# A four-layer graph stack on one core: a delayed linear map in layer 2, one added tile for its sums, small weights made in layer 0, and one running sum instead of two

## The chip, the cores and the metric

The kernel runs on one core of a Trainium2 chip. The metric is device time in microseconds (us) for one execution of the whole program. Two programs are compared: the kernel before and the changed one. A profile of one execution lies beside the times; its clock counts from the first to the last instruction.

## The reference, cut to what matters

`x` is 8 x 2048 x 64 in fp32; `adj` is a 2048 x 2048 row-normalised 0/1 graph. Four pre-norm layers each add something to `x`:

```python
def ln(x): return (x - mean(x, -1)) / sqrt(var(x, -1) + 1e-5)
# layer 0: weights per node n, made from a 16-wide embedding
h = max(ln(x), 0)
T = [h, A @ h, 2 * A @ (A @ h) - h]
w = einsum('nd,dkio->nkio', embedding, weight)      # 2048 x 3 x 64 x 64
x += einsum('bnki,nkio->bno', T, w) + embedding @ bias
# layer 1: three steps of a small network over v and A @ v
v = max(ln(x), 0); v[:, 0] = iv
for _ in range(3):
    v = relu(concat(v, A @ v) @ W1.T + b1) @ W2.T + b2
x += v
# layer 2: linear
h = max(ln(x), 0)
x += ((A @ h) * (w_nl.sum(-1) / sqrt(2)) + b_nl) @ w_out.T + b_out
# layer 3: attention masked by adj > 0.5; with no entry over 0.5
# every row's softmax is uniform, so each row gets the mean of h
h = max(ln(x), 0)
x += elu(mean over nodes of h)
```

## The kernel before, in words

**Two paths.** `uniform_path` computes under the assumption that all non-zero entries of a row of `adj` are equal and at most 0.5, and tests that assumption on the way. `general_path` follows under a branch and isn't taken with these inputs. Everything here is about `uniform_path`.

**Tiling.** Two batch entries of 64 channels form a pair of 128 columns; there are four pairs, `p` = 0 to 3. The nodes are cut into four blocks of 512, `nb` = 0 to 3. The sign of the transposed graph stays in SBUF as `BT`. A product with the graph (`product`, lines 170 to 182) takes one block: 16 chunks `m` of 128 nodes, each with a high and a low part of the operand (`H` and `L`, made by `halves`, lines 162 to 168), so 32 matmuls of 128 x 512 into one PSUM bank; VectorE then multiplies the bank by the row scale `crow` (line 181). `fill` lets a caller issue other work between chunks.

**Layer 0** runs per pair: four products for the first term, four for the second, and after each of these `node_weights` (lines 310 to 343). That function walks over 4 tiles `t` and two groups `dg` of 8 embedding entries. Per group TensorE makes `y` in PSUM (line 328, a tile of two banks, two such tiles), and VectorE adds each of its 8 slices times an embedding column to a sum (line 339). The kernel before keeps two sums: even entries go to `acc`, odd ones to `odd` (line 336 starts it), and line 342 adds them. `keep` then writes `x` to DRAM, normalises (`norm_relu`, lines 140 to 160) and writes `h` to DRAM.

**Norm.** `norm_relu` is a chain over three engines: VectorE sums, scales and subtracts the mean (145 to 147), ScalarE squares (151), VectorE sums and scales (153, 154), GpSimd takes the power -1/2 (156), VectorE applies it with the rectifier (157). Its output tile `z` shares a pool tag of 3 buffers with `hb`, the tile that `load_h` fills.

**Small weights.** After layer 0 its pools are closed. Lines 389 to 449 then load `W1`, `W2`, `w_out` and the vectors by some twenty DMAs on the SP queue into the same memory, transpose and multiply them on TensorE and copy them on VectorE.

**Layer 1** (515 to 565) has 3 steps of 4 products per pair; `back_to_nodes` (454 to 459, tile `bn`) applies a 128 x 128 matrix to a block. In its first two steps `test` (line 495) compares a quarter row of `adj` with the row's maximum; `test_load` fetches those quarters one call ahead into 4 buffers.

**Layer 2 and 3** (569 to 612) have one product per block and then `finish`: the GpSimd adds the bias row to `x` (578), `back_to_nodes` applies the matrix, VectorE adds (580), `norm_relu` follows, and four matmuls with a matrix of ones add the block's `z` over the nodes into the PSUM tile `pS` (583), over all four blocks. After the last block lines 602 to 612 turn `pS` into a row, add it to the four kept `acc` tiles and write the output through the POOL queue.

**Order.** The program is written for a tile framework: it assigns buffers and semaphores, and within each engine it orders the instructions by the place in the program at which they are issued and by its own estimate of when each is ready. So instructions may stand on an engine's queue later or earlier than the source has them[...].

Of the kernel before, what the change touches and what calls it, by code (L numbers as in the profile page):

```python
# [8 lines left out]
F32 = mybir.dt.float32  # L9
F32R = mybir.dt.float32r  # L10
I32 = mybir.dt.int32
U8 = mybir.dt.uint8
# [28 lines left out]
def uniform_path(  # L41
# [98 lines left out]
    def norm_relu(xt, name):  # L140
# [17 lines left out]
            g, g, 0.0, rstd[:, :, None].to_broadcast([P, 8, C]), op0=ALU.max, op1=ALU.mult  # L158
# [113 lines left out]

    l0p = l0.enter_context(tc.tile_pool(name="l0p", bufs=1))
# [36 lines left out]
    def node_weights(p, nb, terms):  # L310
# [3 lines left out]

        odd = l0p.tile([P, 4, 2 * C], F32, name="odd")
        av = acc.rearrange("p j (b c) -> p j b c", b=2)
        ov = odd.rearrange("p j (b c) -> p j b c", b=2)
# [3 lines left out]
        for t in range(4):  # L321
            ts = slice(t * P, (t + 1) * P)
            for dg in range(D // DG):
                y = psum.tile([P, 2, 512], F32, tag="big", name=f"y_{p}_{nb}_{t}_{dg}")
                for k in range(K):
                    for bb in range(2):
                        hs_ = slice(bb * C, (bb + 1) * C)
                        nc.tensor.matmul(  # L328
                            y[:, bb, :], terms[k][hs_, ts], wt[hs_, k, dg * 512:(dg + 1) * 512],
                            start=(k == 0), stop=(k == K - 1),  # L330
                        )
                for d in range(DG):
                    e = dg * DG + d
                    yd, ec = y[:, :, d * C:(d + 1) * C], emb[:, 4 * nb + t, e:e + 1]
                    if e == 1:
                        nc.vector.tensor_scalar(ov[:, t], yd, ec, None, op0=ALU.mult)
                        continue
                    xj = (av, ov)[d % 2][:, t]
                    nc.vector.scalar_tensor_tensor(  # L339
                        xj, yd, ec, xj, op0=ALU.mult, op1=ALU.add  # L340
                    )
        nc.vector.tensor_tensor(acc, acc, odd, op=ALU.add)
        keep(p, nb, acc, f"1_{p}_{nb}")

    for p in range(NP):
# [14 lines left out]
        for nb in range(NB):  # L360
            nm = f"0_{p}_{nb}b"
            crow = load_crow(nb, nm)
# [23 lines left out]
    def feat(name):  # L386
        return lastp.tile([P, 512], F32, tag="fm", name=name, bufs=8)

    def two_halves(src, width, name):
        t = lastp.tile([P, width], F32, name=name)  # L390
        for hf in range(2):
            nc.sync.dma_start(t[hf * C:(hf + 1) * C, :], src)
        return t

    def row(src, name):

        t = lastp.tile([P, 2 * C], F32, name=name)
        nc.sync.dma_start(
            t.rearrange("p (b c) -> p b c", b=2),
            bass.AP(tensor=src.tensor, offset=src.offset, ap=[[0, P], [0, 2], [1, C]]),  # L400
        )
        return t

    def block_diag(src, name):

        t = lastp.tile([P, P], F32, name=f"{name}n")
        nc.vector.memset(t, 0.0)
        for hf in range(2):
            s = slice(hf * C, (hf + 1) * C)
            nc.sync.dma_start(t[s, s], src)  # L410
        ps = bank("tr", f"ps_{name}")
        nc.tensor.transpose(ps[:, :P], t, ident)
        tT = lastp.tile([P, P], F32, name=name)
        nc.vector.tensor_copy(tT, ps[:, :P])
        return t, tT

    def made(name, lhsT, rhs, n=P):
        ps = bank("tr", f"ps_{name}")
        nc.tensor.matmul(ps[:, :n], lhsT, rhs, start=True, stop=True)
        t = lastp.tile([P, n], F32, name=name)  # L420
        nc.vector.tensor_copy(t, ps[:, :n])
        return t

    _, w1vT = block_diag(w1[:, :C], "w1v")
    _, w1eT = block_diag(w1[:, C:], "w1e")
    w2n, w2T = block_diag(w2, "w2")
    _, woT = block_diag(w_out, "wo")
    b1c = two_halves(b1[:, None], 1, "b1c")
    b2c = two_halves(b2[:, None], 1, "b2c")
    bnl = two_halves(b_nl[:, None], 1, "bnl")  # L430
    wn = two_halves(w_nl, 2, "wnl")
    b2r = row(b2, "b2r")
    bor = row(b_out, "bor")
# [3 lines left out]
    w1v2 = made("w1v2", w2n, w1vT)  # L437
    w1e2 = made("w1e2", w2n, w1eT)
    r1e = made("r1e", b2c.to_broadcast([P, P]), w1eT)
    b1s = made("b1s", w1vT, b2c, 1)  # L440
    nc.vector.tensor_tensor(b1s, b1s, b1c, op=ALU.add)

    rbo = made("rbo", bnl.to_broadcast([P, P]), woT)
    nc.vector.tensor_tensor(rbo, rbo, bor, op=ALU.add)
    ws = lastp.tile([P, 1], F32, name="wsum")
    nc.vector.tensor_scalar(wn, wn, INV_SQRT2, None, op0=ALU.mult)
    nc.vector.tensor_tensor(ws, wn[:, 0:1], wn[:, 1:2], op=ALU.add)
    wos = lastp.tile([P, P], F32, name="wos")
    nc.vector.tensor_scalar(wos, woT, ws, None, op0=ALU.mult)
# [32 lines left out]
    tested = []  # L482

    def test_load():
        for _ in range(2):
            i, q = divmod(len(tested), NB)
            st = lastp.tile([P, 512], F32, name="st", bufs=4)
            nc.sync.dma_start(st, adj[i * P:(i + 1) * P, q * 512:(q + 1) * 512])
            tested.append(st)

    def test(k):

        i, q = divmod(k, NB)
        junk = lastp.tile([P, 512], U8, name="junk")
        nc.vector.scalar_tensor_tensor(  # L495
            junk, tested[k], cols[:, i, :], tested[k], op0=ALU.not_equal, op1=ALU.logical_and,
            accum_out=bad[:, i, q:q + 1],
        )
# [16 lines left out]
    def layer1(n, p):  # L515
        hl, gT = ops[n]
        steps = 3
        for s in range(steps):
# [22 lines left out]
            for nb in range(NB):  # L541
# [3 lines left out]
                nc.tensor.matmul(ph, w1v2 if s else w1vT, gT[nb], start=True, stop=True)  # L545
                g = feat(f"g_{nm}")
                product(hl, nb, nm, g, crow, fill={8: mid} if nb == 3 else {})
                nc.vector.tensor_tensor(g, ph, g, op=ALU.add)  # L548
                nc.scalar.activation(g, g, AF.Relu, bias=b1s if s else b1c)  # L549
# [5 lines left out]
                if s < 2:  # L555
                    k = 2 * (8 * p + 4 * s + nb)
                    test(k)
                    test(k + 1)
                    if k + 2 < NCH * NB:
                        test_load()  # L560
# [8 lines left out]
    def layer2(n, p):  # L569
        hl, _ = ops[n]  # L570
        pS = bank("tr", f"pS_{p}")
        accs = []

        def finish(nb, e):
# [4 lines left out]
            pn = back_to_nodes(e, wos, f"2_{p}_{nb}")  # L579
            nc.vector.tensor_tensor(acc, pn, acc, op=ALU.add)  # L580
            z = norm_relu(acc, f"3_{p}_{nb}")
            for t in range(4):
                nc.tensor.matmul(  # L583
                    pS[:, :2 * C], ones, z[:, t, :],
                    start=(nb == 0 and t == 0), stop=(nb == NB - 1 and t == 3),
                )

        for nb in range(NB):
            nm = f"2_{p}_{nb}"
            crow = load_crow(nb, nm)  # L590
            e = product(
                hl, nb, nm, feat(f"e_{nm}"), crow,
                fill={8: lambda: prepare(n + 1, 2)} if nb == 3 else {},
            )
            finish(nb, e)
            if nb in (1, 2):
                prepare(n + 1, nb - 1)
        prepare(n + 1, 3)

# [14 lines left out]
    test_load()  # L614
# [599 lines left out]
```

## Time and profile before

| what | value |
|---|---|
| median of 3 runs | 1420.28 us |
| lowest and highest | 1418.68 and 1424.58 us |
| the profiled execution | 1418.68 us |
| its span, first to last instruction | 1416.9 us |
| TensorE matmul busy | 1277.4 us, 90% |
| VectorE busy | 805.6 us, 57% |
| GpSimd busy | 241.3 us, 17% |
| ScalarE busy | 187.4 us, 13% |
| mean granted TensorE clock | 0.962 |

In the profile PE is TensorE's matmul side and PEld its weight load, DVE VectorE, ACT ScalarE, POOL GpSimd, and SP the engine that issues most DMAs. A group line gives the source line, engine, operation, output and inputs, shape and count; after the first bar the busy time in us and the mean of one in ns; after the second the idle time of that engine just before, and what ended it. A timeline line gives start, duration, and in brackets the idle time before it with what ended it. Fp32 matmuls are recorded as two passes, so one call can show as two records.

By the timeline layer 0 with its prologue takes up to 720, the weights and the restart of layer 1 to 743, layer 1 to 1211, and layers 2 and 3 the rest.

### The profile page before, as it was taken

To read this page: it belongs to the slowest core of one execution; us is meant where nothing else is said; L and a number is where in the kernel's file an instruction comes from. 1 tells how busy PE (TensorE), PEld (TensorE's weight loads), DVE (VectorE), ACT (ScalarE), POOL (GpSimd) and SP (SyncE) were. 2 spreads that over 40 slices of the span, in tenths; PEclk is the share of its full clock that TensorE was granted. 3 is DMA by queue.
4 is the path that set the end of the run, shared out by engine and by line. 5 is a ranking of instruction groups with operands and counts; after the bars stand their busy time and mean duration, and the time that the engine had idled before them with its cause. 6 is when DMAs were issued, how large, how long until landed. Compare 5 with 4: busy or idle time off the path is not lost.

```text
span 1416.9 us, 16169 instructions
## 1 busy us (share of the span) xinstructions
PE 1277.4 (90%) x6000; PEld 899.3 (63%) x6000; DVE 805.6 (57%) x1956; ACT 187.4 (13%) x317; POOL 241.3 (17%) x234
## 2 busy tenths in 40 slices
PE   3899699997999799999949899999999999998883
PEld 2775355854566355755528687778778777776662
DVE  5655677476774777367757845334434433656553
ACT  3540001100100000000001112112112111101100
POOL 1200210212110211102010003002102201333442
PEclk9999899998999999999979999999999999999996
DMA  5771211211211211101027714103102211422220
GB/s 170 235 195 43 74 49 38 86 45 50 74 45 49 75 49 41 49 23 56 31 73 241 247 51 131 38 26 110 67 26 93 83 30 55 132 83 89 97 90 32
DMA packets 92299, 115.86 MB, mean 82 GB/s; under 512 B 50356, under 2 KB 52404, under 8 KB 92212
## 3 DMA queue, kind: packets, MB, share of 16 engines
q1 hardware_dynamic: 80052, 89.03, 21.2%
q0 software_dynamic: 7936, 24.66, 4.6%
q10 hardware_dynamic: 4224, 1.05, 0.3%
q8 instruction: 50, 0.82, 0.2%
q14 instruction: 37, 0.30, 0.1%
HBM read 90.05 MB, written 24.65 MB: 81 GB/s over the span
## 4 chain that ended last, share of the span: by engine, by line
PE 60%; DVE 10%; issue 10%; POOL 6%; DMA 4%; ACT 1%; SPq 1%; POOLq 0%; DVEq 0%; ACTq 0%
PE bv L175 23%; PE y L328 17%; POOL rstd L156 4%; PE bn L458 3%; PE ph L545 3%; DMA st<-in_adj_dram 2%; DVE z L157 2%; PE bv_3a L175 2%; PE bv_2a L175 2%; PE bv_0a L175 2%; PE bv_1a L175 2%; PE bv_0b L175 2%; POOL out_dram L609 1%; PE pS L583 1%; PE bn_u L458 1%
## 5 line engine op out<-in xcount | busy, mean ns | idle before, releaser
L175 PE MATMUL bv<-BT,H 128*128 128x512 f32 x1024 | 422.5, 413 | 0.0
L175 PE MATMUL bv<-BT,L 128*128 128x512 f32 x1024 | 406.2, 397 | 0.4 <-DVE L L167 0.4
L175 PEld LDWEIGHTS bv<-BT,L 128*128 128x128 f32 x1024 | 193.8, 189 | 49.9 <-issue 9.3
L175 PEld LDWEIGHTS bv<-BT,H 128*128 128x128 f32 x1024 | 193.6, 189 | 48.0 <-issue 9.3
L339 DVE SCALAR_TENSOR_TENSOR acc<-y,emb,acc 128x128 f32<-128x128 f32 x512 | 176.5, 345 | 79.7 <-PE y L328 75.3
L328 PE MATMUL y<-wt,t0T 64*128 64x512 f32 x512 | 145.1, 627 | 35.7 <-DVE odd L339 35.7
L339 DVE SCALAR_TENSOR_TENSOR odd<-y,emb,odd 128x128 f32<-128x128 f32 x448 | 153.7, 343 | 0.0
L306 POOL DMA_DIRECT2D xs<-acc x32 | 17.7, 554 | 781.1 <-DVE acc L528 347.9
L156 POOL TENSOR_TENSOR rstd<-var,mhalf 128x8 f32<-128x8 f32 x64 | 106.9, 1671 | 226.5 <-DVE var L154 199.1
L151 ACT ACTIVATE sq<-z 128x512 f32<-128x512 f32 x64 | 40.4, 631 | 627.5 <-DVE z L147 622.6
L157 DVE SCALAR_TENSOR_TENSOR z<-z,rstd 128x512 f32<-128x512 f32 x64 | 53.8, 840 | 107.9 <-POOL rstd L156 107.9
L328 PEld LDWEIGHTS y<-wt,t0T 64*128 64x128 f32 x512 | 46.3, 193 | 102.8 <-issue 101.1
L181 DVE TENSOR_TENSOR g<-bv,crow 128x512 f32<-128x512 f32 x48 | 33.1, 690 | 129.0 <-PE bv L175 128.7
L153 DVE TENSOR_REDUCE var<-sq 128x8 f32<-128x512 f32 x64 | 43.8, 684 | 28.5 <-ACT sq L151 28.5
L495 DVE SCALAR_TENSOR_TENSOR junk<-st,cols 128x512 uint8<-128x512 f32 x64 | 48.6, 759 | 14.4 <-DMA st<-in_adj_dram 13.0
L188 PE MATMUL pt_adj<-ident,st 128*128 128x128 f32 x256 | 39.5, 303 | 16.6 <-DMA st<-in_adj_dram 8.5
L224 DVE TENSOR_REDUCE cols<-st 128x1 f32<-128x1024 f32 x32 | 38.9, 1217 | 23.2 <-DMA st<-in_adj_dram 23.1
L188 PEld LDWEIGHTS pt_adj<-ident,st 128*128 128x128 f32 x256 | 31.8, 155 | 25.8 <-ACT BT L223 15.3
L583 PE MATMUL pS<-z,ones 128*128 128x128 f32 x128 | 20.4, 307 | 30.0 <-DVE z L157 30.0
L549 ACT ACTIVATE g<-g,b1s 128x512 f32<-128x512 f32 x32 | 23.2, 724 | 174.8 <-DVE g L548 174.8
L145 DVE TENSOR_REDUCE mean<-acc 128x8 f32<-128x512 f32 x64 | 43.4, 684 | 4.4 <-DMA acc<-in_x_dram 2.9
L147 DVE TENSOR_TENSOR z<-acc,mean 128x512 f32<-128x512 f32 x64 | 44.1, 694 | 1.7
(186 smaller groups left out, 1841.1 us busy)
## 6 DMA issues: line engine op xcount, KB each, us to landing
st<-in_adj_dram SPq DMA_DIRECT2D x32, 512.0 KB, 4.5
crow<-crowD SPq DMA_DIRECT2D x64, 256.0 KB, 3.3
st<-in_adj_dram SPq DMA_DIRECT2D x64, 256.0 KB, 3.4
hs<-z POOLq DMA_DIRECT2D x44, 256.0 KB, 2.7
hb<-hs SPq DMA_DIRECT2D x44, 256.0 KB, 4.0
xs<-acc POOLq DMA_DIRECT2D x32, 256.0 KB, 2.5
acc<-xs SPq DMA_DIRECT2D x32, 256.0 KB, 3.7
acc<-in_x_dram SPq DMA_DIRECT2D x56, 128.0 KB, 2.7
```

The lines of the kernel that those rows point to most:

```text
L145: nc.vector.tensor_reduce(mean, groups(xt), axis=AX.X, op=ALU.add)
L147: nc.vector.tensor_tensor(g, groups(xt), mean[:, :, None].to_broadcast([P, 8, C]), op=ALU.subtract)
L153: nc.vector.tensor_reduce(var, groups(sq), axis=AX.X, op=ALU.add)
L156: nc.gpsimd.tensor_tensor(rstd, var, mhalf, op=ALU.pow)
L157: nc.vector.scalar_tensor_tensor(g, g, 0.0, rstd[:, :, None].to_broadcast([P, 8, C]), op0=ALU.max, op1=ALU.mult)
L175: nc.tensor.matmul(ps, hl[m // 4][i][:, m % 4, :], BT[:, nb, m, :], start=(m == 0 and i == 0), stop=(m == NCH - 1 and i == 1),)
L188: nc.tensor.transpose(pt[:, t, :], src(t), ident)
L328: nc.tensor.matmul(y[:, bb, :], terms[k][hs_, ts], wt[hs_, k, dg * 512:(dg + 1) * 512], start=(k == 0), stop=(k == K - 1),)
L339: nc.vector.scalar_tensor_tensor(xj, yd, ec, xj, op0=ALU.mult, op1=ALU.add)
L458: nc.tensor.matmul(ps[:, t, :], fT[:, t * P:(t + 1) * P], wmat, start=True, stop=True)
L495: nc.vector.scalar_tensor_tensor(junk, tested[k], cols[:, i, :], tested[k], op0=ALU.not_equal, op1=ALU.logical_and, accum_out=bad[:, i, q: ...
L545: nc.tensor.matmul(ph, w1v2 if s else w1vT, gT[nb], start=True, stop=True)
```

## The change

- `node_weights`: the tile `odd`, its start (336) and the added line 342 go. All 16 entries of a tile `t` are added to the one slice `av[:, t]`, in order.
- The small weights are made by a new function `make_weights`, called in layer 0 for the last pair ahead of the second product of block 1. It uses three `z` buffers, and writes its eight 128 x 128 results to DRAM (`wD`) by two DMAs on the POOL queue. After layer 0 one DMA of 512 KB brings them into `wl`; two loads of `iv` and one row `b2r` stay there. `b1c` is loaded ahead of `make_weights`.
- `test` takes a whole row block: four loads, each followed by its comparison, into 2 buffers, at blocks 0 and 2 of the first two steps; the loads one call ahead go.
- Layer 1 keeps the product in a tile of its own (`e`) ahead of the activation. The tag `fm` has 10 buffers where it had 8.
- Layer 2: `finish(nb - 1)` and a later `prepare` are issued after chunk 4 inside the product of block `nb`. The block's `z` no longer goes through line 583: for block 0 `norm_relu` writes into `zsum`, and for blocks 1 to 3 VectorE adds `z` to it. After the last block four matmuls with ones add up `zsum`.

```diff
 def norm_relu(xt, name, out_=None):
...
-            g, g, 0.0, rstd[:, :, None].to_broadcast([P, 8, C]), op0=ALU.max, op1=ALU.mult
+            g if out_ is None else groups(out_), g, 0.0,
+            rstd[:, :, None].to_broadcast([P, 8, C]), op0=ALU.max, op1=ALU.mult,
...
+    def make_weights():
+        b2c = col(b2[:, None], 1, "b2c")
+        bnl = col(b_nl[:, None], 1, "bnl")
+        wn = col(w_nl, 2, "wnl")
...
+        raw, tr, pr = (block("z", f"wz{i}", 3) for i in range(3))
+        nc.gpsimd.memset(raw, 0.0)
+        for i, w in enumerate((w1[:, :C], w1[:, C:], w2, w_out)):
+            for hf in range(2):
+                hs_ = slice(hf * C, (hf + 1) * C)
+                nc.sync.dma_start(raw[hs_, i, hs_], w)
+        nc.vector.tensor_copy(tr, transposed(lambda t: raw[:, t, :], "wT"))
+        ps = psum.tile([P, 4, P], F32, tag="tr", name="wP")
...
+        for i, (lhsT, rhs) in enumerate(pairs):
+            nc.tensor.matmul(ps[:, i, :], lhsT, rhs, start=True, stop=True)
+        nc.vector.tensor_copy(pr, ps)
...
+        fill_row(raw[:, 0, :], b_out)
+        nc.vector.tensor_tensor(pr[:, 3, :], pr[:, 3, :], raw[:, 0, :], op=ALU.add)
...
+        nc.gpsimd.dma_start(wD[:, 0], tr)
+        nc.gpsimd.dma_start(wD[:, 1], pr)
...
-        odd = l0p.tile([P, 4, 2 * C], F32, name="odd")
...
+                xj = av[:, t]
                 for d in range(DG):
                     e = dg * DG + d
-                    yd, ec = y[:, :, d * C:(d + 1) * C], emb[:, 4 * nb + t, e:e + 1]
-                    if e == 1:
-                        nc.vector.tensor_scalar(ov[:, t], yd, ec, None, op0=ALU.mult)
-                        continue
-                    xj = (av, ov)[d % 2][:, t]
                     nc.vector.scalar_tensor_tensor(
-                        xj, yd, ec, xj, op0=ALU.mult, op1=ALU.add
+                        xj, y[:, :, d * C:(d + 1) * C], emb[:, 4 * nb + t, e:e + 1], xj,
+                        op0=ALU.mult, op1=ALU.add,
                     )
-        nc.vector.tensor_tensor(acc, acc, odd, op=ALU.add)
...
+            if p == NP - 1 and nb == 1:
+                make_weights()
...
+    wl = lastp.tile([P, 2, 4, P], F32, name="wl")
+    nc.sync.dma_start(wl, wD)
...
+    def test(i):
+        for q in range(NB):
+            st = lastp.tile([P, 512], F32, name="st", bufs=2)
+            nc.sync.dma_start(st, adj[i * P:(i + 1) * P, q * 512:(q + 1) * 512])
+            junk = lastp.tile([P, 512], U8, name="junk")
+            nc.vector.scalar_tensor_tensor(
...
-            z = norm_relu(acc, f"3_{p}_{nb}")
-            for t in range(4):
-                nc.tensor.matmul(
-                    pS[:, :2 * C], ones, z[:, t, :],
-                    start=(nb == 0 and t == 0), stop=(nb == NB - 1 and t == 3),
-                )
+            z = norm_relu(acc, f"3_{p}_{nb}", zsum if nb == 0 else None)
+            if nb > 0:
+                nc.vector.tensor_tensor(zsum, zsum, z, op=ALU.add)
+
+        def behind(nb):
+            if nb > 0:
+                finish(nb - 1)
+            if nb > 1:
+                prepare(n + 1, nb - 2)
 
         for nb in range(NB):
...
+            fill = {4: lambda: behind(nb)}
+            if nb == 3:
+                fill[8] = lambda: prepare(n + 1, 2)
+            e.append(product(hl, nb, nm, feat(f"e_{nm}"), crow, fill=fill))
+        finish(3)
         prepare(n + 1, 3)
+        pS = bank("tr", f"pS_{p}")
+        for t in range(4):
+            nc.tensor.matmul(pS[:, :2 * C], ones, zsum[:, t, :], start=(t == 0), stop=(t == 3))
```

## The prediction

> **What bounds the kernel now.** I read the groups first, then busy time by stretch, then the timelines of TensorE and VectorE. The groups that the change touches (busy us, mean ns, then idle before it and what ended that):
>
> ```profile
> L339 DVE SCALAR_TENSOR_TENSOR acc<-y,emb,acc 128x128 f32<-128x128 f32 x512 | 176.5, 345 | 79.7 <-PE y L328 75.3
> L328 PE MATMUL y<-wt,t0T 64*128 64x512 f32 x512 | 145.1, 627 | 35.7 <-DVE odd L339 35.7
> L583 PE MATMUL pS<-z,ones 128*128 128x128 f32 x128 | 20.4, 307 | 30.0 <-DVE z L157 30.0
> ```
>
> In `node_weights` VectorE waits for TensorE's `y` (75.3 us), hardly the other way. In layer 2 it is reversed: TensorE sits idle 30.0 us ahead of the `pS` matmuls, for the norm's last step. By stretch (window, length, then busy us of PE, PEld, DVE, ACT, POOL, clock, DMA):
>
> ```profile
> 610.74:631.68 20.94, 20.94 (x98) 9.58 (x97) 15.82 (x57) 0.00 (x0) 0.00 (x0) 1.00 0.04 14
> 717.80:743.40 25.60, 4.71 (x15) 3.17 (x15) 11.17 (x39) 0.93 (x2) 4.05 (x4) 0.60 0.30 94
> 1210.90:1400.50 189.60, 157.41 (x779) 126.59 (x778) 106.33 (x180) 20.48 (x35) 71.29 (x63) 0.96 0.26 85
> ```
>
> A block's `y` stage is all TensorE (20.94 of 20.94). Between layers 0 and 1 TensorE works 4.71 of 25.60 us. In layer 2 it lacks 32 of 189.6 us. How VectorE's instructions follow each other is what decides; this is its timeline in that `y` stage and at the end of layer 0:
>
> ```profile
> 657.87 0.35 DVE L339 SCALAR_TENSOR_TENSOR acc<-y,emb,acc 128x128 f32<-128x128 f32 x1 [0.46 <-PE y L328]
> 658.13 0.34 DVE L336 TENSOR_SCALAR odd<-y,emb 128x128 f32<-128x128 f32 x1
> 658.39 0.34 DVE L339 SCALAR_TENSOR_TENSOR acc<-y,emb,acc 128x128 f32<-128x128 f32 x1
> ...
> 719.57 0.34 DVE L339 SCALAR_TENSOR_TENSOR odd<-y,emb,odd 128x128 f32<-128x128 f32 x1
> 719.95 0.69 DVE L342 TENSOR_TENSOR acc<-acc,odd 128x512 f32<-128x512 f32 x1
> 720.68 0.69 DVE L145 TENSOR_REDUCE mean<-acc 128x8 f32<-128x512 f32 x1
> ```
>
> Alternating sums start 0.26 us apart although each lasts 0.343: the next starts ahead of the end. Line 342 reads what the instruction before it wrote, and line 145 does too: each starts 0.03 to 0.04 after that end. And layer 2's norm on VectorE:
>
> ```profile
> 1339.02 0.69 DVE L580 TENSOR_TENSOR acc<-bn,acc 128x512 f32<-128x512 f32 x1 [1.34 <-PE bn L458]
> 1342.12 0.69 DVE L153 TENSOR_REDUCE var<-sq 128x8 f32<-128x512 f32 x1 [0.76 <-ACT sq L151]
> 1344.84 1.75 DVE L157 SCALAR_TENSOR_TENSOR z<-z,rstd 128x512 f32<-128x512 f32 x1 [1.82 <-POOL rstd L156]
> 1346.51 1.28 DVE L167 TENSOR_TENSOR L<-hb,H 128x512 fp32r<-128x512 f32 x2
> 1348.07 0.69 DVE L181 TENSOR_TENSOR e<-bv,crow 128x512 f32<-128x512 f32 x1 [0.28 <-PE bv L175]
> ```
>
> The chain takes 7.57 us (1339.02 to 1346.59), of which 2.6 are waits for ScalarE and GpSimd. The product's scaling `e` stands behind it.
>
> **What the Trainium skill says.** "VectorE: DVE Perf Modes", section "The DRAIN you can't avoid": the next op waits for the pipe to empty, a semaphore adds nothing, but one that isn't held starts earlier. The trace agrees with the last clause (0.26 us apart at 0.343 long) and not with the second: a dependent start costs 0.12 us more. "SBUF — State Buffer" states in its single rule on ports that VectorE and GpSimd share a port pair exclusively, and that an op with two SBUF inputs contends. The trace agrees: line 157 lasts 0.69 us alone and 1.75 where GpSimd's line 578 (1344.78, 1.26 us) runs. "TensorE: Matmul & The Clock Gate", Part 1, says that about 3.4 us of idling halves the clock; here after a gap of 3.41 us at 1329 matmuls come 0.43 us apart, not 0.228.
>
> **Part 1, one running sum.** 16 instructions of a tile `t` now each read the one before. A dependent start gives 0.343 + 0.035 = 0.378 us; a group of 8 takes 3.03 us where TensorE makes one in 20.94 / 8 = 2.62. So VectorE becomes the bound of the stage. With two `y` tiles TensorE runs two groups ahead, then goes at VectorE's pace: 2.62 + 6 x 3.03 + 2.62 = 23.4 us a block, 2.5 more. VectorE then finishes 3.3 us later than now, less 0.73 for line 342; the norm behind it takes about 5.8 us, so the next product's scaling, queued behind the norm, is late for a 7.5 us product by some 0.4. I replayed the queue order of the trace with both costs: 2.75 to 2.93 more per block, 45.7 over 16. I take **+46**. Bounds: if dependent starts were free, nothing but the 0.73 us of line 342, mostly behind products (-2); if other work never overlaps, 16 x 8 x 0.41 = +52.
>
> **Part 2, layer 2.** The 16 groups of `pS` become 4. One costs TensorE 0.91 us (1255.34 to the next product matmul at 1256.25): 12 x 0.91 = 11 off its queue. Idle time up to the last `bn` is 25.5 us, matmuls at the halved clock another 8.5. If all goes, TensorE needs 32 x 0.2285 + 0.91 + 0.23 = 8.5 us a block against (1393.6 - 1212.0) / 16 = 11.35 now: -45. But VectorE comes next: chain 7.57, the added sum 0.72, its share of lines 602 to 607 (3.75 / 4), so 9.2 us a block even if `e` and line 167 fit in the 1.82 us wait; line 578 still follows `rstd` on POOL, so the 1.75 stays. 16 x (11.35 - 9.2) = -34. The output's eight POOL DMAs (6.0 us) of one pair meet the next pair's `rstd`: I charge 4 us in all. **-30**; bounds -38 (contention mostly gone) and -12 (`e` stays behind `z` and the added sum: 9.2 + 0.7 + 0.7 = 10.6 a block).
>
> **Part 3, weights.** After layer 0 SP issues 16 fewer small loads of about 0.63 us and one row fewer. The restart waits for the first `hb`: issued at 733.73, landed at 743.04, behind two rows of 64 KB that took 5.6 and 8.0 us to land. Now `wl`, two `iv`, one row: about 2.4 us of issue from 720.1, so `hb` goes at 722.5 not 733.7; the row remains ahead, so I keep 7 to 8 us to landing: 730. **-13** (-8 to -16). TensorE's and VectorE's removed steps lay inside that gap: nothing more.
>
> **Part 4, the same weights inside layer 0.** TensorE gets some 18 records of 0.11 us, 2 us; VectorE two copies of 0.69 and five small ones, 2.6, where Part 1 has made it the bound. Two waits are new on VectorE's queue, with `y` sums behind: `pr` needs a `z` buffer whose DMA (2.5 us) must end, and the `b_out` row must land (5.6 us for a row like it). I charge half of these, 3.5. POOL's memset and two DMAs stand in idle POOL time (21 us gaps). SP's loads are issued during a 21 us `y` stage; the `crow` load behind them has that cover, and without it costs up to 8. **+6** (+2 to +14).
>
> **Part 5, tests.** 64 comparisons remain. Two buffers instead of four: a load lands in 3.5 us, so about 2.3 us a test rather than 1.2, and VectorE's queue waits behind each. Before, TensorE lost 2.69 and 2.89 us here. **+2** (-4 to +12). **Tail:** the added sum lies on the last chain, +0.7. The tile `e` in layer 1 adds no instruction.
>
> **Sum:** 46 - 30 - 13 + 6 + 2 + 1 = +12. From the profiled 1418.7 that is 1430.7; the median lies 1.6 higher, so 1432.
>
> **Rivals.** (a) *Layer 2 becomes TensorE's alone*: the scaling moves into the `rstd` wait and GpSimd's add leaves line 157; -38 in place of -30, with the weights at -14 and little stall: about 1421, no change. For it: 1.82 us of bare wait in each norm; against: line 578 comes straight after `rstd`. (b) *New waits*: `e` stays behind the added sum (-15) and the tests or `b_out` hold VectorE's queue (+10 more): about 1452. For it: waits in queue order cost 30 us now. (c) **Faster**: the dependent chain in `node_weights` is cheaper than a dependent start elsewhere, because VectorE finds the other norms' instructions to put between. Place: line 339; price: at 0.34 us apart a group takes 2.72 us and Part 1 falls to about 16 x (6 x 0.10 + 0.4) = 16, so 1402. It decides from 0.36 us apart downward, where Part 1 is under 34. Against it: the chain's groups follow each other with nothing else ready in pair 3. (d) The change doing nothing is excluded: `pS` records must fall by 96.
>
> **Chances.** Forecast 0.45 (1422 to 1442), (a) 0.22, (b) 0.18, (c) 0.15. Within 0.5%, about what a measurement here tells from no change, is 1413 to 1427: (a), with a little of the forecast and less (c): 0.26. Faster 0.15, slower 0.59. The range reaches to the middle of (c) and just past that of (b), 1402 to 1455, and so leaves out about half of each, 0.17.
>
> **What would show it.** Line 339 starting 0.38 us apart with TensorE waiting for it over 100 us (Part 1); `y` stages of 23 to 24 us; few gaps before `pS`, layer 2 ending its last `bn` some 150 us after its start (Part 2); the first `pt` of layer 1 about 13 us after the last `y`, not 25 (Part 3); idle VectorE ended by `b_out`'s DMA (Part 4). Starts 0.26 us apart in line 339 would break the forecast.

## The result and the profile after

| | before | after |
|---|---|---|
| median | 1419.48 us | 1468.05 us |
| lowest and highest | 1414.11 and 1424.58 us | 1467.40 and 1475.08 us |
| span of the profiled execution | 1416.9 us | 1465.5 us |

These are four runs of each; the median of before stood at 1420.28 when there were three. The ratio of the times is 1.0354, with a 95% interval of 1.0304 to 1.0404: the change makes the kernel 3.5% slower. The forecast was 1432 with a range up to 1455, so the sign was right and the size was not: 48.6 us of span came where the sum said 12.

The spans can be cut at the same instructions in both traces (last `y` matmul, first transpose of layer 1, last linear map `bn` of layer 1, last `bn` of layer 2):

| stage | before | after | difference | the sum said |
|---|---|---|---|---|
| up to the first `y` matmul's end | 121.1 | 120.3 | -0.8 | 0 |
| layer 0, to the last `y` | 596.6 | 654.2 | +57.6 | +52 (Parts 1 and 4) |
| between layers 0 and 1 | 25.7 | 14.3 | -11.4 | -13 (Part 3) |
| layer 1 | 471.4 | 481.4 | +10.0 | +2 (Part 5) |
| layer 2, to the last `bn` | 179.0 | 171.4 | -7.6 | -30 (Part 2) |
| behind the last `bn` | 23.0 | 23.8 | +0.8 | +1 (tail) |

Two rows miss by much: layer 2 by 22 us and layer 1 by 8. Layer 0 misses by 6. First the groups on the page of the kernel after, in the same columns as before:

```profile
L383 DVE SCALAR_TENSOR_TENSOR acc<-y,emb,acc 128x128 f32<-128x128 f32 x1024 | 355.3, 350 | 62.8 <-PE y L376 20.2
L376 PE MATMUL y<-wt,t0T 64*128 64x512 f32 x512 | 149.1, 646 | 68.1 <-DVE acc L383 65.1
L482 DVE SCALAR_TENSOR_TENSOR junk<-st,cols 128x512 uint8<-128x512 f32 x64 | 48.6, 759 | 48.4 <-DMA st<-in_adj_dram 47.9
```

The wait between the two engines has turned round: VectorE now waits 20.2 us for `y` (75.3 before), TensorE 65.1 us for VectorE (35.7 before). The third line is the tests of layer 1: VectorE stands 47.9 us for their inputs, where it stood 13.0 before.

VectorE's part of one block of layer 0, where nothing else stands between:

```profile
648.31 24.58 DVE L383 SCALAR_TENSOR_TENSOR acc<-y,emb,acc 128x128 f32<-128x128 f32 x64 [2.10 <-PE y L376]
```

The same 64 instructions took 20.3 us before (613.63 to 633.94 in its timeline), and line 342 another 0.7. The busy time by stretch, in the columns of the forecast's table, for the `y` stage of that block, the stretch between the layers and layer 2:

```profile
645.42:669.76 24.34, 22.49 (x98) 9.63 (x97) 20.06 (x57) 0.00 (x0) 0.00 (x0) 1.00 0.04 12
774.50:788.80 14.30, 0.00 (x0) 0.00 (x0) 5.97 (x16) 0.93 (x2) 4.06 (x4) 0.67 0.52 153
1266.30:1448.30 182.00, 149.97 (x683) 120.88 (x682) 112.29 (x191) 19.72 (x35) 71.75 (x63) 0.92 0.27 89
```

The `y` stage grew from 20.94 to 24.34 us and TensorE lacks 1.85 of it. In layer 2 TensorE had 32.2 us idle before (189.60 less 157.41) and has 32.0 now (182.00 less 149.97): the forecast had most of that idle time go, and none did. What went is TensorE's own work, the 96 records of `pS`.

What TensorE waits for between the two `bn` marks shows where the wait is now. Before:

```profile
PE pS L583 <- DVE z L157: 23.4, 15, 3.4
PE bn L458 <- DVE e L181: 1.9, 2, 1.2
```

After:

```profile
PE bn L452 <- DVE e L182: 19.5, 9, 4.1
PE bv L176 <- DVE L L168: 4.7, 1, 4.7
PE pS L585 <- DVE zsum L566: 0.9, 1, 0.9
```

The columns are us in total, times, longest. The 23.4 us ahead of `pS` are gone but for 0.9, and 19.5 us ahead of `bn`, for the scaling `e`, and one wait of 4.7 us for `L` stand in their place. The timeline of VectorE in the last pair of the kernel after, with GpSimd's addition of the bias row put in at its time, says why:

```profile
1424.99 0.17 DVE L154 TENSOR_SCALAR var<-var 128x8 f32<-128x8 f32 x1
1426.91 1.26 POOL L561 TENSOR_TENSOR acc<-acc,wl 128x512 f32<-128x512 f32 x1
1426.97 1.74 DVE L157 SCALAR_TENSOR_TENSOR z<-z,rstd 128x512 f32<-128x512 f32 x1 [1.82 <-POOL rstd L156]
1428.64 0.68 DVE L182 TENSOR_TENSOR e<-bv,crow 128x512 f32<-128x512 f32 x1
1429.24 0.68 DVE L566 TENSOR_TENSOR zsum<-zsum,z 128x512 f32<-128x512 f32 x1
1430.63 0.69 DVE L563 TENSOR_TENSOR acc<-bn,acc 128x512 f32<-128x512 f32 x1 [0.72 <-PE bn L452]
```

TensorE had ended that product's matmuls at 1423.9 and the first ten of the next product, which stand ahead of `bn` on its queue, at 1426.2. Then it could go no further:

```profile
1429.37 0.82 PE L452 MATMUL bn<-wl,e 128*128 128x128 f32 x5 [3.21 <-DVE e L182]
```

The scaling could have run from 1423.9 and starts at 1428.64: it stands behind line 157, which first waits 1.82 us for GpSimd's `rstd` and then takes 1.74. That closes a loop: `e` of a block behind the norm of the block before it on VectorE, `bn` behind `e`, and the next norm behind `bn`. The one wait of 4.7 us for `L` has the same origin: line 168 (167 before), which makes it, starts at 1350.57, behind a line 157 that had waited 1.82 us for `rstd` and taken 1.74 (from 1348.18).

### The profile page after: what moved, and what is told of

It reads as the page before. It is cut to its first block, busy times and chain, and to the rows that moved or that the text cites. A ratio compares the mean times of both kernels' runs of the same rounds, so it can differ in the third digit from the quotient of the medians.

```text
span 1465.5 us, 15962 instructions
## 1 busy us (share of the span) xinstructions
PE 1292.0 (88%) x5904; PEld 893.5 (61%) x5904; DVE 878.3 (60%) x1941; ACT 186.7 (13%) x317; POOL 243.3 (17%) x237
## 3 DMA queue, kind: packets, MB, share of 16 engines
q1 hardware_dynamic: 80196, 89.55, 20.1%
## 4 chain that ended last, share of the span: by engine, by line
PE 35%; DVE 24%; issue 17%; DMA 8%; POOL 6%; ACT 1%; DVEq 0%; POOLq 0%; SPq 0%; ACTq 0%
PE bv L176 19%; DVE acc L383 15%; DMA st<-in_adj_dram 6%; POOL rstd L156 4%; PE bn L452 3%; PE y L376 3%; PE ph L532 2%; DVE junk L482 2%; PE bv_0a L176 2%; PE bv_1a L176 1%; PE bv_3a L176 1%; PE bv_2a L176 1%; PE bv_0b L176 1%; DVE mean L145 1%; DVE var L153 1%
## 5 line engine op out<-in xcount | busy, mean ns | idle before, releaser
L176 PE MATMUL bv<-BT,H 128*128 128x512 f32 x1024 | 422.4, 413 | 0.3 <-ACT H L167 0.3
L383 DVE SCALAR_TENSOR_TENSOR acc<-y,emb,acc 128x128 f32<-128x128 f32 x1024 | 355.3, 350 | 62.8 <-PE y L376 20.2
L376 PE MATMUL y<-wt,t0T 64*128 64x512 f32 x512 | 149.1, 646 | 68.1 <-DVE acc L383 65.1
L182 DVE TENSOR_TENSOR e<-bv,crow 128x512 f32<-128x512 f32 x64 | 44.1, 689 | 124.3 <-PE bv L176 124.2
L482 DVE SCALAR_TENSOR_TENSOR junk<-st,cols 128x512 uint8<-128x512 f32 x64 | 48.6, 759 | 48.4 <-DMA st<-in_adj_dram 47.9
L452 PE MATMUL bn<-wl,g 128*128 128x128 f32 x384 | 51.6, 277 | 7.9 <-ACT g L536 7.3
L452 PEld LDWEIGHTS bn<-wl,g 128*128 128x128 f32 x384 | 49.4, 192 | 14.0 <-ACT g L536 10.3
L189 PEld LDWEIGHTS pt_adj<-ident,st 128*128 128x128 f32 x256 | 32.0, 155 | 25.6 <-ACT BT L224 15.4
L536 ACT ACTIVATE g<-e,b1s 128x512 f32<-128x512 f32 x32 | 23.2, 724 | 165.2 <-DVE e L534 165.1
```

What stands on the lines that cost most here:

```text
L176: nc.tensor.matmul(ps, hl[m // 4][i][:, m % 4, :], BT[:, nb, m, :], start=(m == 0 and i == 0), stop=(m == NCH - 1 and i == 1),)
L182: nc.vector.tensor_tensor(out, ps, crow, op=ALU.mult)
L189: nc.tensor.transpose(pt[:, t, :], src(t), ident)
L376: nc.tensor.matmul(y[:, bb, :], terms[k][hs_, ts], wt[hs_, k, dg * 512:(dg + 1) * 512], start=(k == 0), stop=(k == K - 1),)
L383: nc.vector.scalar_tensor_tensor(xj, y[:, :, d * C:(d + 1) * C], emb[:, 4 * nb + t, e:e + 1], xj, op0=ALU.mult, op1=ALU.add,)
L452: nc.tensor.matmul(ps[:, t, :], fT[:, t * P:(t + 1) * P], wmat, start=True, stop=True)
```

## Experiments

Times are medians beside the kernel before on the same chip, with the ratio to it. "More" and "less" than the changed kernel compare with its median of 1468.05, which was not measured beside them; the kernel before, which was, has medians between 1418.2 and 1421.1 us there. Only `u_sum`, `l2_dep` and the three kernels put together have intervals clear of the changed kernel's (1.0304 to 1.0404). For the others the stretches of the traces, one profiled execution each, have to carry the reading. "Idle" is TensorE's, between the two `bn` marks of layer 2.

### Layer 0: is it the dependency?

`u_sum`: the two sums back, nothing else.

```diff
-                xj = av[:, t]
...
+                    xj = (av, ov)[d % 2][:, t]
...
+        nc.vector.tensor_tensor(acc, acc, odd, op=ALU.add)
```

> The changed kernel with the sum over a node's neighbours in layer 0 put back into two sums, neighbours taken alternately, and the adding of the two put back too; all else as changed. Theory (each of the 16 multiply-adds reads the sum that the one ahead of it wrote, and waits for that): the y stages of layer 0 fall from about 24.5 to about 21 us, the starts of the multiply-adds stand 258 ns apart and not 386, and 48 us go: about 1420. Rival (VectorE is bound by how many instructions it has, or by what they read, so one sum costs no more than two): no change or slower, 1468 to 1475.

Measured: 1412.62 us, ratio 0.9945 (0.9924 to 0.9967). On its page:

```profile
L389 DVE SCALAR_TENSOR_TENSOR acc<-y,emb,acc 128x128 f32<-128x128 f32 x512 | 175.9, 344 | 78.7 <-PE y L378 72.1
L378 PE MATMUL y<-wt,t0T 64*128 64x512 f32 x512 | 146.9, 626 | 36.1 <-DVE odd L389 36.1
```

VectorE waits 72.1 us for `y` again, and the median distance of two starts is 258 ns. The stretches of `y` matmuls (cut where they pause over 5 us) take 372.6 us together, 422.4 in the changed kernel, 366.3 before. That is 50 us for the one sum; all of layer 0 gives 51 (603.0 and 654.2), the medians 55. All the rest of the change together makes the kernel 0.3 to 0.8% faster.

`u_split`: two sums, but eight neighbours in a row to each.

```diff
-                xj = av[:, t]
...
+                    if e == DG:
...
+                    xj = (av, ov)[dg][:, t]
...
+        nc.vector.tensor_tensor(acc, acc, odd, op=ALU.add)
```

> The changed kernel with two sums in layer 0, but the first eight neighbours go to one and the last eight to the other, so that every multiply-add but one still follows the one whose sum it reads; the two are added at the end. Theory of the dependency: the starts stay 386 ns apart, and the time is 1460 to 1480. Rival (two tiles by themselves, or less in one tile, are what made the kernel before quick): about 1420, as with alternate sums.

Measured: 1482.24 us, ratio 1.0427 (1.0390 to 1.0465). Its timeline:

```profile
505.43 0.35 DVE L386 TENSOR_SCALAR odd<-y,emb 128x128 f32<-128x128 f32 x1
505.81 2.67 DVE L389 SCALAR_TENSOR_TENSOR odd<-y,emb,odd 128x128 f32<-128x128 f32 x7
508.52 0.69 DVE L392 TENSOR_TENSOR acc<-acc,odd 128x512 f32<-128x512 f32 x1
```

Seven take 2.67 us: (2.67 - 0.35) / 6 = 0.387 us apart, as with one sum (median 386 ns in both). The same instructions on the same two tiles go at 258 or at 386 ns by order alone. So it is the reading of the sum just written, and the rival (two tiles by themselves) falls. Whether the program's semaphore or the engine itself holds the second instruction is not shown. The time lies 14 us over the changed kernel and 2 over the expected range; the added line, 16 x 0.7 = 11 us, is most of the 14.

### Layer 1: two buffers

`t_bufs4`: four buffers for the tests' inputs, and one `fm` buffer fewer for room.

```diff
-    return lastp.tile([P, 512], F32, tag="fm", name=name, bufs=10)
+    return lastp.tile([P, 512], F32, tag="fm", name=name, bufs=9)
...
-            st = lastp.tile([P, 512], F32, name="st", bufs=2)
+            st = lastp.tile([P, 512], F32, name="st", bufs=4)
```

> The changed kernel with four buffers in place of two for the input lists that the tests of layer 1 read, paid for with one output buffer fewer. Theory (with two buffers VectorE waits 48 us for the transfers in layer 1, 13 us before, and that is most of the 10 us that layer 1 grew): 6 to 10 us less, about 1459. Rival (what costs is where in VectorE's order the tests stand, or the second half of the setup that waits behind them): no change, 1465 to 1471.

Measured: 1462.28 us, ratio 1.0301 (1.0266 to 1.0336), 5.8 us less than the changed kernel. VectorE's waits in layer 1:

```profile
DVE junk L482 <- DMA st<-in_adj_dram: 16.2, 19, 3.2
```

They were 47.9. Layer 1 takes 474.0 us where it took 481.4, so the buffers are 7.4 of its 10.0 (in the kernels with two buffers it takes 480.8 to 484.7, in the four with four 473.1 to 475.8). The other 2.6 were not pursued.

### The weights

`u_w`: the weights made behind layer 0 again, `make_weights` and `wD` gone.

```diff
-            if p == NP - 1 and nb == 1:
-                make_weights()
...
+    _, w1vT = block_diag(w1[:, :C], "w1v")
...
+    wos = lastp.tile([P, P], F32, name="wos")
+    nc.vector.tensor_scalar(wos, woT, ws, None, op0=ALU.mult)
```

> The changed kernel with the later weights made after layer 0 again, as in the kernel before (one output buffer fewer, for room). By the traces the junction between the layers fell by 11 to 14 us and layer 0 grew by 6 to 8: 3 to 8 us more than the changed kernel, 1471 to 1476. Rival (making them inside layer 0 costs as much as it saves): 1465 to 1470.

Measured: 1475.79 us, ratio 1.0395 (1.0354 to 1.0435), 7.7 us more than the changed kernel. The stretch between the layers is 23.9 us, against 14.3 in the changed kernel and 11.3 to 12.6 in the other kernels with early weights. The `y` stage that holds `make_weights` takes 32.7 us in the changed kernel and 24.7 here; with two sums it is 27.0 against 21.2. So the early weights save 10 to 13 between the layers and cost 6 to 8 in that stage. Over all of layer 0 the two profiles differ by only 1.6 us (654.2 and 652.6), so what they cost outside that stage is not pinned down. The two waits that the forecast named, in the changed kernel's timeline:

```profile
682.59 0.69 DVE L305 COPY wz<-pt_wT 128x512 f32<-128x512 f32 x1 [2.58 <-PE pt_wT L189]
685.75 0.69 DVE L311 COPY wz<-wP 128x512 f32<-128x512 f32 x1 [2.47 <-DMA hs<-z]
```

The wait for a `z` buffer came (2.47 us); the one for the `b_out` row did not, and one for the transposes (2.58 us) stood in its place.

### Layer 2: which wait holds it?

`u_l2`: layer 2 of the kernel before in the changed kernel.

```diff
-            fill = {4: lambda: behind(nb)}
...
+            finish(nb, e)
+            if nb in (1, 2):
+                prepare(n + 1, nb - 1)
```

> The changed kernel with layer 2 of the kernel before (each block's linear map and norm straight after its own product, the sums of h by TensorE after each block). From the traces, layer 2 and the tail fell by about 7 us with the change, where the prediction said 29. If that reading is right: 5 to 9 us slower than the changed kernel, 1473 to 1477. Rival (the new order gains what was predicted, and something else in the changed kernel lies on layer 2 and hides it): about 1497.

Measured: 1476.41 us, ratio 1.0422 (1.0377 to 1.0466), 8.4 us more. Its layer 2 takes 181.8 us, against 171.4. The new layer 2 is worth 8 to 10 us, and nothing else hides a larger gain.

`l2_noadd`: one link of the loop shortened, by leaving the row out.

```diff
-            nc.gpsimd.tensor_tensor(acc, acc, rows4(rbo), op=ALU.add)
```

> The changed kernel without GpSimd's addition of the row of w_out and b_nl in layer 2, so that the output lacks that row: one link of the chain from norm to norm is shortened, since the last multiplication of the norm takes 1.75 us where that addition lies on it and 0.69 where it doesn't. Theory (layer 2 is held by the loop of scaling, linear map and norm, TensorE waits 19.5 us in it): 8 to 15 us less, 1453 to 1460. Rival (layer 2 is held by the loads of x and of the counts, or by TensorE itself): 1464 to 1470.

Measured: 1454.81 us, ratio 1.0265 (1.0222 to 1.0308), 13.2 us less. Line 157 takes 0.69 us in each of layer 2's norms; in the changed kernel nine of the 16 take 1.74 to 1.78. TensorE's waits for `e` fall from 19.5 to 10.4 us. That fits the loop, but also GpSimd's additions as the bound: the later finish was to tell.

`l2_far`: the finish of a block behind the next product.

```diff
-            fill = {4: lambda: behind(nb)}
...
+            while late:
+                late.pop(0)()
+            late.append(lambda nb=nb: finish(nb))
```

> The changed kernel with the finish of a layer 2 block (linear map, norm, output) issued one product later, so that VectorE's scaling of the next block stands ahead of the norm of this one in its queue. Theory (the changed layer 2 is a loop: scaling behind norm on VectorE, product behind scaling, norm behind product): the 173 us of layer 2 fall to about 150, and the time to 1443 to 1450. Rival (GpSimd's additions and the output transfers hold layer 2): 1464 to 1472.

Measured: 1466.65 us, ratio 1.0335 (1.0299 to 1.0370): no change. TensorE's wait for `e` fell from 19.5 to 3.3 us and the stretch by 10.5, but two norms were left behind the last product, and the end of the span came 32.0 us after the last `bn` instead of 23.8.

`l2_far2`: the same with the third finish inside the last product.

```diff
+                fill={8: lambda: prepare(n + 1, 2) if n + 1 < len(items) else flush()} if nb == 3 else {},
```

> As with the finish of each layer 2 block one product later, but in the last pair the finish of the third block stands inside the fourth product, so that one norm and not two is left behind the last product. In the trace of the one before, the stretch of layer 2 to the last linear map fell by 10.5 us and the tail behind it grew by 8.2. Theory (both readings right): 8 to 11 us less than the changed kernel, 1457 to 1460. Rival (what the stretch gained was the clock, or it comes back as a wait on x or on the next pair's halves): 1463 to 1469.

Measured: 1465.47 us, ratio 1.0324 (1.0282 to 1.0366): again no change. GpSimd's timeline in the last pair:

```profile
1424.21 5.99 POOL L602 DMA_DIRECT2D out_dram<-acc  x8 [1.62 <-DVE acc L600]
1430.23 3.71 POOL L567 TENSOR_TENSOR acc<-acc,wl 128x512 f32<-128x512 f32 x3
```

Three additions stand behind the eight output transfers of the pair before; VectorE waits 5.2 us for the first. In the whole stretch GpSimd's additions wait another 32.1 us for loads of x, up to 9.0 at a time; in the changed kernel no such wait shows.

`l2_sp` and `l2_far3`: those transfers sent by SP's queue, in the changed kernel and in `l2_far2`.

```diff
-                nc.gpsimd.dma_start(
+                nc.sync.dma_start(
                     out[2 * p + bb].rearrange("(j p) c -> p j c", p=P)[:, part(nb), :],
```

> The changed kernel with the output of layer 2 sent off by SP's queue in place of GpSimd's, which takes 6.0 us to issue a pair's eight transfers, with its additions for the next block behind them. If those six us hold the first blocks of a pair: 3 to 8 us less, 1460 to 1465. Rival (they lie beside other work, or SP's own queue is held as long as GpSimd's was): 1466 to 1472.

> The kernel with the finish of each layer 2 block one product later and the short end, and the output sent off by SP's queue. In the trace of the one without that, VectorE waited 5.2 us in the last pair for an addition that GpSimd had behind the eight output transfers, and 4.6 of that came back as a wait of TensorE's last linear map. Theory (the later finish took the loop away, and the output transfers took its place): 1451 to 1458. Rival (TensorE and the start of each pair hold it): 1462 to 1467.

Measured: `l2_sp` 1463.80 us, ratio 1.0318 (1.0279 to 1.0356), 4.3 less than the changed kernel, within the expected 3 to 8 but not clear of its spread. `l2_far3` 1464.31 us, ratio 1.0306 (1.0270 to 1.0343): the theory fell. GpSimd's additions there waited 53.0 us for the loads of x, up to 10.2 at a time; those loads stand in SP's queue. So putting the finish a whole product later trades the loop for waits in other queues. It does not show that the loop costs nothing.

`l2_dep`: only VectorE's order in the loop. The norm's last multiplication and the added sum are issued behind the next product, and since the order on the queue is planned from estimated times, a dependency forces it: the multiplication takes its lower limit, zero, from zero times a column of the next `e`.

```diff
+                    floor = small.tile([P, 1], F32, name="floor")
+                    nc.vector.tensor_scalar(floor, e[nb + 1][:, 0:1], 0.0, None, op0=ALU.mult)
...
+            if rests:
+                rests.pop()()
...
-                g if out_ is None else groups(out_), g, 0.0,
+                g if out_ is None else groups(out_), g, floor,
```

> The changed kernel with one thing more: in layer 2 the last multiplication of a block's norm takes its lower limit of zero from a one-column product of zero and the next block's scaled product, so that VectorE's order, which is planned from estimates, has to put the next block's scaling ahead of that multiplication, into the wait for GpSimd. Where loads, additions and outputs stand stays as it is. Theory of the loop (scaling behind norm, linear map behind scaling, norm behind linear map): TensorE's 19.5 us of waits for the scaling mostly go, and 10 to 15 us with them: 1453 to 1458. Rival (GpSimd's additions, the loads of x or the granted clock take it back, as with the finish one product later): 1462 to 1468.

Measured: 1452.11 us, ratio 1.0221 (1.0180 to 1.0263), 15.9 us less than the changed kernel. Its timeline, at the same block as shown above (the third of the last pair):

```profile
1419.46 0.17 DVE L154 TENSOR_SCALAR var<-var 128x8 f32<-128x8 f32 x1
1419.54 0.69 DVE L188 TENSOR_TENSOR e<-bv,crow 128x512 f32<-128x512 f32 x1
1420.27 0.15 DVE L576 TENSOR_SCALAR floor<-e 128x1 f32<-128x1 f32 x1
1421.45 1.76 DVE L159 SCALAR_TENSOR_TENSOR z<-z,floor,rstd 128x512 f32<-128x512 f32 x1 [1.03 <-POOL rstd L156]
```

and what TensorE waits for:

```profile
PE pS L603 <- DVE zsum L579: 7.7, 3, 2.6
PE bn L458 <- DVE e L188: 6.1, 5, 1.8
```

The scaling lies in the wait for `rstd`, whose remaining bare part is 1.03 us. From this scaling to the next of the pair are 8.31 us (the next starts at 1427.85), where the changed kernel takes 10.21 (1428.64 to 1438.85). The waits for `e` fall from 19.5 to 6.1 us and that for `L` from 4.7 to 0.2; those ahead of `pS` rise from 0.9 to 7.7. GpSimd's addition still lies on the multiplication (1.76). Only this order was changed, so the loop is shown to have held back these 16 us.

The stretch of layer 2 by its parts (one profiled execution each; the last column runs to the end of the span):

| kernel | length | TensorE busy | idle | clock | behind it |
|---|---|---|---|---|---|
| before | 179.0 | 153.5 | 25.6 | 0.97 | 23.0 |
| after | 171.4 | 146.1 | 25.4 | 0.93 | 23.8 |
| `l2_noadd` | 156.1 | 140.7 | 15.3 | 0.98 | 24.0 |
| `l2_far` | 160.9 | 142.0 | 18.9 | 0.96 | 32.0 |
| `l2_far2` | 161.6 | 142.6 | 18.9 | 0.96 | 29.1 |
| `l2_far3` | 163.0 | 142.9 | 20.1 | 0.95 | 30.5 |
| `l2_dep` | 152.5 | 138.4 | 14.1 | 0.98 | 26.7 |

### The row elsewhere, and kernels put together

`l2_xs`: the row added where layer 1 stores x.

```diff
-                    keep(p, nb, acc, f"2_{p}_{nb}")
+                    ax = lastp.tile([P, 4, 2 * C], F32, name="ax", bufs=1)
+                    nc.gpsimd.tensor_tensor(ax, acc, rows4(rbo), op=ALU.add)
+                    nc.gpsimd.dma_start(xs[p][:, part(nb), :], ax)
...
-            nc.gpsimd.tensor_tensor(acc, acc, rows4(rbo), op=ALU.add)
```

> The changed kernel with the row of w_out and b_nl added by GpSimd when layer 1 stores x, and not in layer 2, so that layer 2 has no addition of GpSimd beside the norm's last multiplication and the output is whole. Theory (the gain of leaving the row out came from that link of the loop, and the last stage of layer 1 has room for 16 additions): 1454 to 1459. Rival (the addition slows the norm of layer 1's last stage by as much): 1464 to 1470.

Measured: 1462.18 us, ratio 1.0298 (1.0263 to 1.0332): 5.9 us less than the changed kernel, between the two theories. Layer 1 takes 481.7 us, as without it (481.4), so layer 1 takes nothing back. Layer 2 takes 162.3, though its instructions are those of `l2_noadd`, which took 156.1. TensorE's waits for `e` are the same (10.5 and 10.4 us), so the loop gained as much. Of the difference, 2.9 us are matmul time, at a clock of 0.95 in place of 0.98, and 3.4 idle, one wait at the handover from layer 1:

```profile
1274.26 1.27 POOL L517 TENSOR_TENSOR ax<-acc,wl 128x512 f32<-128x512 f32 x1 [3.37 <-DMA xs<-ax]
1277.19 0.69 DVE L157 SCALAR_TENSOR_TENSOR z<-z,rstd 128x512 f32<-128x512 f32 x1 [3.44 <-POOL rstd L156]
1278.54 0.80 PE L176 MATMUL bv<-BT,L 128*128 128x512 f32 x1 [3.43 <-DVE L L168]
```

The tile `ax` has one buffer, so GpSimd waits for its last transfer, the norm's `rstd` stands behind that, and the operands of the first product behind the norm. A second buffer was not tried.

`best`, `best2` and `best6` put the pieces together: two sums, four buffers, early weights, and in layer 2 the late finish, the row moved, or the row moved and the order forced.

> Two sums in layer 0, four buffers for the tests' inputs, the weights made in layer 0, and layer 2 with the finish one product later and the short end. If the pieces add up (1412.6 with two sums, 6 less from the buffers, 8 to 11 less in layer 2): 1394 to 1400, about 0.985 of the kernel before. If the gains in layer 2 don't hold: 1404 to 1412.

> Two sums in layer 0, four buffers for the tests' inputs, the weights made in layer 0, layer 2 ordered as in the changed kernel, and its row added where layer 1 stores x. If the pieces add up (1412.6 with two sums, 6 less from the buffers, 12 less from the row): 1392 to 1398. If layer 1 takes the row's cost back: 1402 to 1408.

> Two sums, four buffers, early weights, the row of layer 2 added where layer 1 stores x, and the order in layer 2 forced as in the run beside this one. If the gains are one and the same (TensorE is the bound once the loop is short): 1392 to 1397, as without the forced order. If they add: 1385 to 1391.

Measured: `best` 1398.34 us, ratio 0.9856 (0.9817 to 0.9895). `best2` 1396.22, ratio 0.9827 (0.9790 to 0.9863). `best6` 1381.08, ratio 0.9744 (0.9701 to 0.9786): 40 us under the kernel before. In `best6` layer 2 takes 149.1 us with 10.4 idle, so the two gains there add.

## Why the prediction was wrong, point by point

**Part 1 (+46) was right in mechanism and some 4 to 10 us short.** With the weights late in both kernels, layer 0 takes 652.6 us in `u_w` and 596.6 before: 56; by the `y` stretches with and without two sums it is 50. Two terms are mis-sized. The dependent start was taken as 0.343 + 0.035 = 0.378 us, and it is 0.386, for an instruction that lasts 0.350 in the chain: over 16 blocks x 6 groups x 8 that is 6.1 us. And VectorE was to finish a block 3.3 us later, where its 64 instructions take 24.6 us in place of 20.3, 4.3 more; 64 x 0.378 = 24.2 would already have been 3.9 more. These overlap and other work hides part of them. Rival (c), a cheaper chain, is excluded by the 386 ns themselves.

**Part 2 (-30) is the step that failed.** It took "9.2 us a block even if `e` and line 167 fit in the 1.82 us wait". They did not. The same paragraph gave the other case, "`e` stays behind `z` and the added sum: 9.2 + 0.7 + 0.7 = 10.6 a block"; the trace has 171.4 / 16 = 10.7. That the two agree so well is in part luck: the average holds the starts of the pairs too, and in the block shown `e` stands behind `z` but ahead of the added sum. The choice between the two was never argued from the trace, although the timeline shown in the forecast already had `e` behind line 157 there. `l2_dep` puts the scaling where the forecast had assumed it and gets 152.5 / 16 = 9.5 a block. So 9.2 was a fair price for an order that the kernel does not have. Nor did the idle time fall: 25.6 and 25.4. The gain of 7.6 is TensorE's busy time, 153.5 to 146.1. The 96 records fewer at 0.114 would be 11 us; the rest goes with the lower clock, 0.93 in place of 0.97. The forecast's 8.5 us for matmuls at the halved clock is too large as well: a mean clock of 0.97 over 179.0 us can have cost some 5. It stands only in the limit of -45.

**Part 3 (-13)** gave -11.4, and -9.6 by `u_w`. **Part 4 (+6)** gave 6 to 8. The two together were forecast at -7 and measured at -7.7 by the medians, whose intervals overlap.

**Part 5 (+2)** gave +10, inside its bounds (-4 to +12). The reason was named, VectorE's queue behind each load, and its price hardly charged: VectorE's waits for `st` rose from 13.0 to 47.9 us, and the forecast let nearly all of that lie beside other work. `t_bufs4` shows that 7.4 of the layer's growth came from it.

**The signs.** Starts of line 383 are 0.386 us apart (0.38 was named), but TensorE waits 65.1 us for it and not over 100; `y` stages take 24.3 to 25.3 us where nothing interrupts them (23 to 24). Layer 2 ends its last `bn` 171.4 us after its start, not 150. The first transpose of layer 1 comes 14.3 us after the last `y` (13), and no wait of VectorE ends with `b_out`.

**Rivals.** (b) is what came, in layer 2 and in the tests at once, with Part 1 some 4 to 10 us larger on top; it had 0.18, and its 1452 was still 16 us short. The forecast and (a) rested on `e` going ahead of line 157 in VectorE's queue. Had (b)'s order been taken in the forecast itself (-12 for -30, +10 for +2), the same sum would have said about 1458.

## What to carry to other kernels

When work is moved behind the next product, write down the order of the in-order engine that results and close the loop through the other engine before pricing it: a gain that depends on an instruction filling a wait exists only if that order puts it there. If the order is planned from estimates, a small true dependency can force it, as in `l2_dep` (moving the issue alone was not run). Where VectorE is as close to being the bound as here, a running sum is cheaper in two alternating tiles than in one, even with an extra addition at the end.

## What the runs showed of the hardware

A 128 x 128 multiply-add of 0.35 us starts 258 ns after the one before it when that wrote another tile, and 386 ns when it reads that one's sum; this holds over 1024 instructions, and with the same tiles in another order (`u_split`). The Trainium skill, "VectorE: DVE Perf Modes", section "The DRAIN you can't avoid", says that the next op does not start until the pipe is empty, and that one which isn't held starts earlier. The two distances agree with these two cases: 386 ns is 36 after the end of an instruction of 350, 258 is 85 ahead of the end of one of 343. That reading the sum just written makes the difference is what the runs add. The forecast set the 0.12 us between them against the page's clause on semaphores; that clause compares copies with and without one, which no run here does.

Some of the idle time in layer 2 cost twice. `l2_dep` has the same matmuls as the changed kernel there (657 and 658 records), and TensorE is busy 138.4 us in place of 146.1, at a granted clock of 0.98 in place of 0.93. Of the 18.9 us by which the stretch fell, 11.3 were idle and 7.7 the matmuls themselves. The sum of the idle time is not what decides: before has 25.6 us of it at a clock of 0.97, after 25.4 at 0.93. The length of single gaps differs: before has one of over 2.7 us (3.41), after has five (2.9 to 4.7), `l2_dep` none (its longest is 2.6). That agrees with "TensorE: Matmul & The Clock Gate", Part 1, by which about 3.4 us of idling lowers the clock. It is read from one profiled execution each, and was not tried by itself.
